# A decoder on one NeuronCore: cross attention by pairs of heads, one local exponential per tile, and other prices in the planner

## The chip, the cores and the metric

The kernel runs on one core of a Trainium2 chip. The metric is the device time of one execution in microseconds. The time before is the median of three runs.

## The reference

1,024 tokens (4 batches of 256) with 256 features pass through six blocks, each on a layer norm of the running sum `x` and added to it: a linear attention with decay, four experts chosen by token number, a product-key memory of 2,025 rows, a local attention, a cross attention, and a mixture of sixteen experts. The change concerns the fourth and fifth:

```python
# local attention: 8 heads of 64, blocks of 16 tokens, causal within a block
qh = einsum('bsd,dhk->bshk', qb, wq) + bq        # kh, vh alike
scores = where(causal, einsum('bqhk,bshk->bhqs', qh / sqrt(64), kh), -1e9)
ctx = einsum('bhqs,bshk->bqhk', softmax(scores), vh)
# cross attention: 16 heads of 16, all 1024 tokens of the context
attn = softmax(einsum('bhqd,bhkd->bhqk', fq_sym(q * scale), fq_sym(k)))
out = einsum('bhqk,bhkd->bhqd', fq_unsigned(attn), fq_sym(v)) @ Wp + bp
```

`fq_sym` and `fq_unsigned` round to 8 bits and back.

## The kernel before

The tokens lie in eight tiles of 128, one token to a partition. Everything up to the mixture of experts is written as Python generators ("streams") that yield wherever another stream may take over: `front(b)` for each batch (the first three blocks up to the indices of the memory), `fetches` (512 indirect DMAs on POOL, 64 for each tile, in 64 groups of eight with three `g` buffers), `weigh` (DVE multiplies and sums the fetched rows with `hb`, ACT takes a tanh, PE adds the weighted rows into `accs` by 16 matmul instructions of 128*32), `turn` and `free` (change of memory pools), `locals_`, `all_queries`, three copies of `units`, `cross_out` and `routes`.

**The order** is written out while the program is built. `Clock.weave` keeps a modelled time for every engine and repeatedly runs the stream whose next step can start first (ties go by rank). `Clock.note` prices each instruction from its shape; `COLUMN` is the price of a column of TensorE in microseconds, 0.00085 at first and 0.0015 from the turn on. On the chip each engine works off its queue in that order; the prices only set the order. A group of fetches may be issued once the group three ahead of it has been added up, and is taken to have landed 8 us after its issue.

**Cross attention** works a unit (a tile and a head) at a time. PE makes the scores, 128 x 1,024, by two bf16 matmuls with 64 rows of contraction (a head's 16 features in several bf16 terms); even heads lie on partitions 0 to 63 and odd ones on 64 to 127. DVE takes the maximum `mx` and a bias `nb`; ACT writes the exponential `e` as 8-bit integers, with its row sums; PE transposes `e` (four 8-bit values at a time as f32), ACT spreads it to bf16 (`qqT`), and PE adds eight products with `vi` into `accs`. Three streams `units(k, 3)` take every third unit. Scores need two adjoining PSUM banks. After the turn seven banks are shared: two such pairs, and three single ones for everything else. A unit gives its pair back after its exponential. Tile t+1 may add into `accs` once `cross_out` has taken tile t's sums (`ao`). Queries of tile t need its local attention, and their buffers the end of cross attention of tile t-2; local attention needs the tile's gathered sum.

**Local attention** of a tile computes all 128 x 128 scores of a head in f32 and masks all but the token's own block of 16. `qh` and `kh` hold even heads on partitions 0 to 63 and odd heads on 64 to 127; two forked streams `half(0)` and `half(1)` each do scores, mask, maximum, four exponentials with row sums, division, four transposes and four products for their four heads.

After `weave` comes the mixture of experts: sorting by expert (from line 1257), 24 row tiles by `up` and `down`, and the gathering of the two results of every token, on an order that does not come from the planner.

The names and lines that matter: `Clock.note` (line 81), `Banks.find` (176), `turn` (828), `local_attention` (902), `units` (1051), the list of streams (1241). In the profile every planned instruction has line 77, the helper that records it, so groups are told apart by tile names.

Of the kernel before, what the change touches and what calls it, by code (L numbers as in the profile page):

```python
# [21 lines left out]
P = 128  # L22
D = 256
NT = 8
# [27 lines left out]
class Clock:  # L52
# [4 lines left out]
    COLUMN = 0.00085  # L57
# [9 lines left out]
    class _Engine:  # L67
# [3 lines left out]
        def __getattr__(self, op):  # L71
            emit = getattr(self.engine, op)

            def timed(*args, **kw):
                out = args[0] if args else kw["out"]
                self.clock.note(self.name, op, out, args, kw)
                return emit(*args, **kw)  # L77

            return timed

    def note(self, engine, op, out, args, kw):
# [81 lines left out]
class Banks:  # L163
# [12 lines left out]
    def find(self, n):  # L176
# [3 lines left out]
        sets = self.pairs if n == 2 else [(k,) for k in self.free if k >= self.single]  # L180
# [24 lines left out]
def decoder(ctx, tc, a, out):  # L205
# [622 lines left out]
    def turn():  # L828
# [12 lines left out]
        A.bk = load(wb, "bk", [P, 4])  # L841
        A.wv = load(wb, "wv", [AW + 1, AH * AW])
# [5 lines left out]
        A.work = ctx.enter_context(tc.tile_pool(name="work", bufs=1))  # L848
        A.q3 = A.work.tile([P, XH, 4, XD], BF16, name="q3", tag="q3")
# [11 lines left out]
        ck.COLUMN = 0.0015  # L861
# [40 lines left out]
    def local_attention(t):  # L902
# [537 lines left out]
```

## Time and profile before

| | |
|---|---|
| Median of three runs | 1300.18 us (1290.26 to 1305.13) |
| The profiled execution | 1261.94 us, span 1260.2 us |
| Mean granted TensorE clock | 0.708 |
| Indices of the first tile ready / first gather | 111 / 112 us |
| Turn of the memory pools | about 404 us |
| First cross scores / last write of `ao` | 493 / 1117 us |
| Last gather issued / last gathered sum added | 971 / 998 us |
| Sorting by expert begins / experts' first gather | 1137 / 1147 us |

In a group's line the columns are: line, engine, operation, tile written <- tiles read, shapes and count; then busy time and mean ns of one; then the engine's idle time just before them and what ended it. In a table of stretches each engine has its busy time and the number of instructions; then follow the granted clock, the DMA engines' busy share and GB/s. An f32 matmul shows as two instructions, a transpose as one. Ends of matmuls are modelled, so PE's busy time is a guide more than a measure.

### The profile page before, as it was taken

How to read it: one execution, taken by the hardware profiler on the slowest of the kernel's cores; microseconds unless marked ns; L12 is line 12 of the kernel's file. 1: busy time of each engine (PE TensorE's matmuls, PEld its weight loads, DVE VectorE, ACT ScalarE, POOL GpSimd, SP SyncE). 2: the span in 40 equal slices, each digit the busy share in tenths (PEclk: the TensorE clock that was granted, in tenths of full speed). 3: DMA queues.
4: the chain of work that ended last, by engine and by line, in shares of the span. 5: the costliest groups of instructions: out<-in, count | busy, mean ns of one | idle time of the engine just before them, and what ended most of it. 6: DMA issues, size and time to landing. Idle time of an engine off the chain costs nothing. (4 is left out here: it accounts for less than half of the span.)

```text
span 1260.2 us, 15565 instructions
## 1 busy us (share of the span) xinstructions
PE 846.4 (67%) x4945; PEld 520.3 (41%) x4945; DVE 821.5 (65%) x2437; ACT 514.4 (41%) x1039; POOL 571.3 (45%) x589
## 2 busy tenths in 40 slices
PE   4672488627834686765688677676786699856990
PEld 3561365414622464333345334343353365323550
DVE  5568667596578458896677775767776767633222
ACT  1241033302301143453575643757456586731220
POOL 2003656575566556576465664655665000002314
PEclk8885588857965877565667866667777566556995
DMA  5012456666556446668665564555665230001323
GB/s 200 1 39 58 135 140 168 188 169 165 138 162 173 134 134 168 172 175 251 167 173 160 162 182 134 149 147 145 179 168 159 87 136 1 5 4 47 84 65 107
DMA packets 68640, 164.67 MB, mean 131 GB/s; under 512 B 15131, under 2 KB 32780, under 8 KB 68557
## 3 DMA queue, kind: packets, MB, share of 16 engines
q0 software_dynamic: 34688, 105.94, 29.9%
q1 hardware_dynamic: 33868, 57.72, 16.6%
q8 instruction: 40, 0.66, 0.2%
q14 instruction: 44, 0.35, 0.1%
HBM read 156.93 MB, written 6.68 MB: 130 GB/s over the span
## 5 line engine op out<-in xcount | busy, mean ns | idle before, releaser
L77 POOL DMA_INDIRECT g<-in_table,idxT x512 | 524.7, 1025 | 438.2 <-issue 153.4
L77 DVE TENSOR_REDUCE mx<-bank 128x1 f32<-128x1024 f32 x128 | 155.8, 1217 | 65.9 <-PE bank L77 51.7
L77 ACT ACTIVATE e<-bank,nb,qs_q 128x1024 uint8<-128x1024 f32 x128 | 154.3, 1206 | 56.1 <-DVE nb L77 22.0
L77 PE MATMUL accs<-g,blk 128*32 128x256 f32 x1024 | 103.9, 542 | 96.5 <-DVE blk L77 69.8
L77 ACT CAST qqT<-bank 128x1024 bf16<-128x1024 uint8 x128 | 127.6, 1010 | 87.9 <-PE bank L77 52.1
L77 PE MATMUL bank<-kT,qT 64*128 64x512 bf16 x256 | 104.2, 518 | 20.8 <-ACT e L77 15.4
L1312 POOL DMA_INDIRECT xr<-xs,smap x24 | 22.7, 948 | 189.5 <-DVE smap L1299 148.4
L77 PEld LDWEIGHTS accs<-g,blk 128*32 128x32 f32 x1024 | 34.5, 141 | 147.3 <-DVE blk L77 77.1
L77 PE MATMUL bank<-ident,e 128*128 128x128 f32 x256 | 72.6, 387 | 32.1 <-ACT e L77 19.0
L77 PE MATMUL accs<-vi,qqT 128*128 128x16 bf16 x1024 | 47.5, 174 | 56.6 <-ACT qqT L77 34.9
L77 DVE TENSOR_TENSOR g<-g,hb 128x1024 f32<-128x1024 f32 x64 | 78.3, 1223 | 8.7 <-issue 5.5
L77 PEld LDWEIGHTS <-qqT 128*128 128x128 bf16 x1024 | 39.8, 103 | 103.7 <-ACT qqT L77 58.9
L77 DVE TENSOR_REDUCE z<-g 128x8 f32<-128x1024 f32 x64 | 78.1, 1220 | 2.2
L77 PEld LDWEIGHTS bank<-ident,e 128*128 128x128 f32 x256 | 36.0, 185 | 85.6 <-issue 35.1
L77 ACT ACTIVATE th<-u 128x16 f32<-128x16 f32 x64 | 13.9, 218 | 90.8 <-DVE u L77 82.0
L77 PE MATMUL bank<-ident,ln_xn 128*128 128x128 f32 x96 | 25.0, 378 | 33.3 <-ACT ln_xn L77 17.1
L77 ACT ACTIVATE ln_xn<-x,ln_nmr,ln_rstd 128x256 f32<-128x256 f32 x48 | 27.0, 595 | 37.4 <-DVE ln_nmr L77 33.1
L77 PE MATMUL bank<-xnT,w_w_up 128*128 128x256 f32 x128 | 35.8, 441 | 7.6 <-ACT xnT L77 4.3
L1321 PE MATMUL ph<-w,xrT 128*128 x96 | 38.9, 513 | 1.8 <-DVE xrT L1318 1.7
L77 PE MATMUL bank<-w_ctxT,aT 128*128 128x256 f32 x128 | 34.3, 421 | 6.7 <-issue 5.1
L77 DVE TENSOR_SCALAR nb<-mx,nsq,ln 128x1 f32<-128x1 f32 x128 | 34.9, 273 | 4.6
L1325 DVE TENSOR_TENSOR hd<-hd,ph 128x176 f32<-128x176 f32 x24 | 8.0, 337 | 42.9 <-ACT hd L1324 42.9
(293 smaller groups left out, 1686.3 us busy)
## 6 DMA issues: line engine op xcount, KB each, us to landing
hb<-hdram SPq DMA_DIRECT2D x128, 256.0 KB
g<-in_table,idxT POOLq DMA_INDIRECT x512
w<-in_w SPq DMA_DIRECT2D x16, 352.0 KB
ys<-yr SPq DMA_DIRECT2D x24, 128.0 KB
w_w2a<-in_w SPq DMA_DIRECT2D x1, 2048.0 KB
x<-in_x SPq DMA_DIRECT2D x8, 128.0 KB
w_ctxT<-in_ctxT SPq DMA_DIRECT2D x1, 1024.0 KB
w_w_up<-in_w_up SPq DMA_DIRECT2D x1, 1024.0 KB
```

The lines of the kernel that those rows point to most:

```text
L77: return emit(*args, **kw)
L1312: nc.gpsimd.indirect_dma_start(out=xr, out_offset=None, in_=xs, in_offset=bass.IndirectOffsetOnAxis(ap=smap[:, i:i + 1], axis=0))
L1321: nc.tensor.matmul(ph.rearrange("p j n -> p (j n)"), xrT[:, k, :], w13[:, bass.ds(e, 1), k, :], start=(k == 0), stop=(k == 1))
L1325: nc.vector.tensor_tensor(hd, hd, ph[:, 1, :], ALU.mult)
```

## The change

Cross attention takes heads by pairs. A unit is now a tile and two heads; it waits until all four banks of the two bank pairs are free, takes them, and issues the four score matmuls with the heads alternating, so that neighbours use different halves of the array's rows. Then it forks into two streams `weighted_sum`, one for each head, which do what followed before. Two streams of pairs take the place of three of single heads. `mx` and `nb` have six buffers in place of four, `e` six in place of three.

Local attention is one stream for all eight heads. The products with `wqk`, the scores and the products with `vh` are issued with their two halves alternating. The masked scores are reduced, by a maximum over the eight blocks of columns, to the 16 columns that belong to the token's own block (`sc`, 128 x 8 x 16); subtracting the maximum, the exponential, the sum and the division happen there, and a product with the 0/1 mask `seen` spreads the result out to 128 columns again. `qh` gets its bias and factor in one instruction with a bias `bq8` that is scaled beforehand, and `cT` is copied whole.

The planner's prices change: `COLUMN` is 0.000525 and then 0.0006, an f32 product is priced at four columns each of at least 128, a transpose in f32 at three, products of 32 output rows at one, bf16 at one; products marked `halves` at 0.55 of that; ACT and DVE prices depend on tensors given as scalars and on row sums.

```diff
-    COLUMN = 0.00085
+    COLUMN = 0.000525
...
                 out = args[0] if args else kw["out"]
                 self.clock.note(self.name, op, out, args, kw)
+                kw.pop("halves", None)
                 return emit(*args, **kw)
...
         n, late = math.prod(out.shape[1:]), 0.11
         if engine == "tensor":
-            wide = (args[2] if op == "matmul" else args[1]).dtype == F32
-            cost, late = max(0.11, n * self.COLUMN) if wide else max(0.03, n * self.COLUMN / 2), 0.17
-            if out.shape[0] == 32:
-                cost = max(0.06, n * self.COLUMN / 4)
+            late = 0.17
+            wide, c = (args[2] if op == "matmul" else args[1]).dtype == F32, self.COLUMN
+            if not wide:
+                cost = max(0.03, n * c)
+            elif op == "transpose":
+                cost = 3 * n * c
+            elif out.shape[0] == 32:
+                cost = n * c
+            else:
+                cost = 4 * c * max(n, P)
+            if kw.pop("halves", False):
+                cost *= 0.55
         elif engine == "scalar":
             scaled, summed = hasattr(kw.get("scale"), "tensor"), "accum_out" in kw
-            cost = 0.06 + n * 0.00083 + 0.23 * (scaled or summed) + 0.06 * (scaled and summed)
+            cost = 0.07 + n * 0.00083 + 0.12 * (scaled or hasattr(kw.get("bias"), "tensor")) + 0.2 * summed
         elif engine == "gpsimd":
             cost = 1.23
         elif op in ("max", "max_index", "tensor_reduce"):
             src = args[1] if op != "max_index" else args[2]
-            cost = (0.15 if op == "max_index" else 0.085) + 0.00104 * math.prod(src.shape[1:])
+            cost = (0.24 if op == "max_index" else 0.085) + 0.00104 * math.prod(src.shape[1:])
         elif op == "reciprocal":
             cost = 0.05 + 0.0064 * n
         elif op == "tensor_tensor_scan":
             cost = 0.1 + 0.0022 * n
+        elif op in ("tensor_scalar", "tensor_copy"):
+            cost = 0.085 + 0.09 * sum(hasattr(x, "tensor") for x in args[2:]) + 0.00054 * n
         else:
-            cost = 0.085 + (0.00054 if op in ("tensor_scalar", "tensor_copy") else 0.00104) * n
+            cost = 0.085 + 0.00104 * n
...
-        sets = self.pairs if n == 2 else [(k,) for k in self.free if k >= self.single]
+        sets = (self.pairs if n == 2 else [sum(self.pairs, ())] if n == 4 else
+                [(k,) for k in self.free if k >= self.single])
...
+        A.bq8 = wb.tile([P, 4], F32, name="bq8", tag="bq8")
+        nc.vector.tensor_scalar(A.bq8, A.bq, 0.125, None, ALU.mult)
...
+        A.seen = A.work.tile([P, P // ABLK, ABLK], F32, name="seen", tag="seen")
+        nc.vector.tensor_scalar(A.seen, cmask, -0.5, None, ALU.is_ge)
...
-        ck.COLUMN = 0.0015
+        ck.COLUMN = 0.0006
...
         se_.activation(vT[0:AW, :], pqk[0:AW, 1, :], AF.Identity, bias=A.conv_bv)
         bank.give(pqk)
         yield "tensor", None
+
+        p = []
+        for part in range(2):
+            p.append((yield from bank.take([P, 4, P])))
+        for m in range(4):
+            for part in range(2):
+                lo = part * AW
+                te_.matmul(p[part][:, m, :], A.wqk[lo:lo + AW, m * P:(m + 1) * P], qk[lo:lo + AW, :],
+                           start=True, stop=True, halves=True)
+        yield "vector", None
+
         qh = work.tile([P, 4, P], F32, name="qh", tag="qh")
+        ve_.scalar_tensor_tensor(qh, p[0], 0.125, bc(A.bq8, 2, P), ALU.mult, ALU.add)
+        bank.give(p[0])
         kh = work.tile([P, 4, P], F32, name="kh", tag="kh")
-        for part, lo in ((0, 0), (1, AW)):
-            p = yield from bank.take([P, 4, P])
-            for m in range(4):
-                te_.matmul(p[:, m, :], A.wqk[lo:lo + AW, m * P:(m + 1) * P], qk[lo:lo + AW, :], start=True, stop=True)
-            yield "vector", None
-            if part == 0:
-
-                for m in range(4):
-                    ve_.tensor_scalar(qh[:, m, :], p[:, m, :], A.bq[:, m:m + 1], 0.125, ALU.add, ALU.mult)
-            else:
-                ve_.tensor_tensor(kh, p, bc(A.bk, 2, P), ALU.add)
-            bank.give(p)
-            yield "tensor", None
+        ve_.tensor_tensor(kh, p[1], bc(A.bk, 2, P), ALU.add)
+        bank.give(p[1])
+        yield "tensor", None
+
+        psc = []
+        for o in range(2):
+            psc.append((yield from bank.take([P, 4, P])))
+        for m in range(4):
+            for o in range(2):
+                te_.matmul(psc[o][:, m, :], qh[o * AW:(o + 1) * AW, m, :], kh[o * AW:(o + 1) * AW, m, :],
+                           start=True, stop=True, halves=True)
+        yield "vector", None
+        pr = work.tile([P, AH, P // ABLK, ABLK], F32, name="pr", tag="pr")
+        for o in range(2):
+            ve_.tensor_tensor(pr[:, 4 * o:4 * o + 4].rearrange("p m g j -> p m (g j)"), psc[o],
+                              bc(cmask.rearrange("p g j -> p (g j)"), 1, 4), ALU.add)
+            bank.give(psc[o])
+
+        sc = work.tile([P, AH, ABLK], F32, name="sc", tag="sc")
+        ve_.tensor_reduce(sc, pr.rearrange("p h g j -> p h j g"), AX.X, ALU.max)
+        sm = work.tile([P, AH], F32, name="sm", tag="sm")
+        ve_.tensor_reduce(sm, sc, AX.X, ALU.max)
+        ve_.tensor_tensor(sc, sc, bc(sm, 2, ABLK), ALU.subtract)
+        yield "tensor", None
         pv = yield from bank.take([P, AH * AW])
         te_.matmul(pv, vT, A.wv, start=True, stop=True)
         yield "scalar", None
+        se_.activation(sc, sc, AF.Exp)
         vh = work.tile([P, AH * AW], F32, name="vh", tag="vh")
         se_.copy(vh, pv)
         bank.give(pv)
-        cT = work.tile([P, 4, P], F32, name="cT", tag="cT")
-
-        def half(o):
-
-            psc = yield from bank.take([P, 4, P])
-            for m in range(4):
-                te_.matmul(psc[:, m, :], qh[o * AW:(o + 1) * AW, m, :], kh[o * AW:(o + 1) * AW, m, :], start=True, stop=True)
-            yield "vector", None
-            pr = work.tile([P, 4, P], F32, name="pr", tag="pr", bufs=2)
-            ve_.tensor_tensor(pr, psc, bc(cmask.rearrange("p g j -> p (g j)"), 1, 4), ALU.add)
-            bank.give(psc)
-            nm = work.tile([P, 4], F32, name="nm", tag="nm", bufs=2)
-            ve_.tensor_reduce(nm, pr, AX.X, ALU.max, negate=True)
-            yield "scalar", None
-            sm = work.tile([P, 4], F32, name="sm", tag="sm", bufs=2)
-            for m in range(4):
-                se_.activation(pr[:, m, :], pr[:, m, :], AF.Exp, bias=nm[:, m:m + 1], accum_out=sm[:, m:m + 1])
-            yield "vector", None
-            ve_.reciprocal(sm, sm)
-            ve_.tensor_tensor(pr, pr, bc(sm, 2, P), ALU.mult)
-            yield "tensor", None
+        yield "vector", None
+        ve_.tensor_reduce(sm, sc, AX.X, ALU.add)
+        ve_.reciprocal(sm, sm)
+        ve_.tensor_tensor(sc, sc, bc(sm, 2, ABLK), ALU.mult)
+        ve_.tensor_tensor(pr, bc(sc, 2, P // ABLK), bc(A.seen, 1, AH), ALU.mult)
+        yield "tensor", None
+        prf = pr.rearrange("p h g j -> p h (g j)")
+        prT = []
+        for o in range(2):
             tp = yield from bank.take([P, 4, P])
             for m in range(4):
-                te_.transpose(tp[:, m, :], pr[:, m, :], ident)
+                te_.transpose(tp[:, m, :], prf[:, 4 * o + m, :], ident)
             yield "scalar", None
-            prT = work.tile([P, 4, P], F32, name="prT", tag="prT", bufs=2)
-            se_.copy(prT, tp)
+
+            prT.append(work.tile([P, 4, P], F32, name="prT", tag=("qh", "kh")[o]))
+            se_.copy(prT[o], tp)
             bank.give(tp)
             yield "tensor", None
-            pc = yield from bank.take([P, 4, P])
-            for m in range(4):
+        pc = yield from bank.take([P, 4, P])
+        for m in range(4):
+            for o in range(2):
                 h = 2 * m + o
-                te_.matmul(pc[o * AW:(o + 1) * AW, m, :], vh[:, h * AW:(h + 1) * AW], prT[:, m, :], start=True, stop=True)
-            yield "scalar", None
-            se_.copy(cT[o * AW:(o + 1) * AW], pc[o * AW:(o + 1) * AW])
-            bank.give(pc)
-
-        yield "tensor", None
-        yield from ck.fork(half(0), half(1))
+                te_.matmul(pc[o * AW:(o + 1) * AW, m, :], vh[:, h * AW:(h + 1) * AW], prT[o][:, m, :],
+                           start=True, stop=True, halves=True)
+        yield "scalar", None
+        cT = work.tile([P, 4, P], F32, name="cT", tag="cT")
+        se_.copy(cT, pc)
+        bank.give(pc)
         yield "tensor", None
...
     def units(k, n):
 
+
+        for j in range(k, NT * XH // 2, n):
+            t, c = 2 * j // XH, j % (XH // 2)
+            yield "tensor", lambda: qready.get(t)
+            while bank.find(4) is None:
+                yield "tensor", (bank, 4)
+            psc = []
+            for o in range(2):
+                psc.append((yield from bank.take([P, T], n=2)))
+            for n_ in range(2):
+                for o in range(2):
+                    hr = slice(o * 64, o * 64 + 64)
+                    te_.matmul(psc[o][:, n_ * 512:(n_ + 1) * 512], QT[t][hr, c, :], kT[hr, c, n_ * 512:(n_ + 1) * 512],
+                               start=True, stop=True, halves=True)
+            yield "vector", None
+            yield from ck.fork(*[weighted_sum(t, 2 * c + o, psc[o]) for o in range(2)])
+
+    def weighted_sum(t, h, psc):
         work = A.work
-        for j in range(k, NT * XH, n):
-            t, h = j // XH, j % XH
-            yield "tensor", lambda: qready.get(t)
-            o, c = h % 2, h // 2
-            hr = slice(o * 64, o * 64 + 64)
-            psc = yield from bank.take([P, T], n=2)
-            for n_ in range(2):
-                te_.matmul(psc[:, n_ * 512:(n_ + 1) * 512], QT[t][hr, c, :], kT[hr, c, n_ * 512:(n_ + 1) * 512],
-                           start=True, stop=True)
-            yield "vector", None
-            mx = work.tile([P, 1], F32, name="mx", tag="mx", bufs=4)
-            ve_.tensor_reduce(mx, psc, AX.X, ALU.max)
-            nb = work.tile([P, 1], F32, name="nb", tag="nb", bufs=4)
-            ve_.tensor_scalar(nb, mx, NSQ[t][:, h:h + 1], ln255, ALU.mult, ALU.add)
-            yield "scalar", None
-
-            e = work.tile([P, T], U8, name="e", tag="e", bufs=3)
-            se_.activation(e, psc, AF.Exp, bias=nb, scale=SQ[t][:, h:h + 1], accum_out=SUMS[t][:, h:h + 1])
-            bank.give(psc)
-
-            yield "tensor", lambda: None if weighted[0] == 2 else 0.0 if t == 0 else summed.get(("o", t - 1))
-            weighted[0] += 1
-
-            tp = yield from bank.take([P, 2, P])
-            for o in range(2):
-                te_.transpose(tp[:, o, :], e.bitcast(F32)[:, o * P:(o + 1) * P], ident)
-            yield "scalar", None
-            qqT = work.tile([P, 8, P], BF16, name="qqT", tag="qqT", bufs=2)
-            se_.copy(qqT.rearrange("p (o j) q -> p o j q", o=2), tp.bitcast(U8).rearrange("p o (q j) -> p o j q", j=4))
-            bank.give(tp)
-            yield "tensor", None
-            for s in range(NT):
-                te_.matmul(accs[:, 1, h * XD:(h + 1) * XD], qqT[:, s, :], vi[:, s, h * XD:(h + 1) * XD],
-                           start=False, stop=(s == NT - 1), skip_group_check=True)
-            weighted[0] -= 1
-            nunits[t] += 1
-            if nunits[t] == XH:
-                summed[("x", t)] = ck.end
+        mx = work.tile([P, 1], F32, name="mx", tag="mx", bufs=6)
+        ve_.tensor_reduce(mx, psc, AX.X, ALU.max)
+        nb = work.tile([P, 1], F32, name="nb", tag="nb", bufs=6)
+        ve_.tensor_scalar(nb, mx, NSQ[t][:, h:h + 1], ln255, ALU.mult, ALU.add)
+        yield "scalar", None
+
+        e = work.tile([P, T], U8, name="e", tag="e", bufs=6)
+        se_.activation(e, psc, AF.Exp, bias=nb, scale=SQ[t][:, h:h + 1], accum_out=SUMS[t][:, h:h + 1])
+        bank.give(psc)
...
-                  Stream(weights()), Stream(locals_()), Stream(all_queries(), rank=0), *[Stream(after_turn(units, k, 3)) for k in range(3)],
+                  Stream(weights()), Stream(locals_()), Stream(all_queries(), rank=0), *[Stream(after_turn(units, k, 2)) for k in range(2)],
```

More of the change, by code (lines that the diff above doesn't have):

```diff
@@ new lines, in weighted_sum @@
+    def weighted_sum(t, h, psc):
+        work = A.work
+        mx = work.tile([P, 1], F32, name="mx", tag="mx", bufs=6)
[6 more added lines that the diff above has]
+        bank.give(psc)
+        yield "tensor", lambda: None if weighted[0] == 2 else 0.0 if t == 0 else summed.get(("o", t - 1))
+        weighted[0] += 1
+        tp = yield from bank.take([P, 2, P])
+        for o in range(2):
+            te_.transpose(tp[:, o, :], e.bitcast(F32)[:, o * P:(o + 1) * P], ident)
+        yield "scalar", None
+        qqT = work.tile([P, 8, P], BF16, name="qqT", tag="qqT", bufs=2)
+        se_.copy(qqT.rearrange("p (o j) q -> p o j q", o=2), tp.bitcast(U8).rearrange("p o (q j) -> p o j q", j=4))
+        bank.give(tp)
+        yield "tensor", None
+        for s in range(NT):
+            te_.matmul(accs[:, 1, h * XD:(h + 1) * XD], qqT[:, s, :], vi[:, s, h * XD:(h + 1) * XD],
+                       start=False, stop=(s == NT - 1), skip_group_check=True)
+        weighted[0] -= 1
+        nunits[t] += 1
+        if nunits[t] == XH:
+            summed[("x", t)] = ck.end
```

## The prediction

> **What bounds the kernel now.** I read the page's busy shares first, then the busy time of each engine between the ends of neighbouring tiles' cross attention (the writes of `ao`), then the groups, the waits, and the chain.
>
> ```profile
> PE 846.4 (67%) x4945; PEld 520.3 (41%) x4945; DVE 821.5 (65%) x2437; ACT 514.4 (41%) x1039; POOL 571.3 (45%) x589
> ...
> core 0: us, PE busy (x) PEld busy (x) DVE busy (x) ACT busy (x) POOL busy (x), PEclk, DMA share, GB/s
> 490.00:591.00 101.00, 64.01 (x432) 33.65 (x432) 85.82 (x264) 47.89 (x96) 67.14 (x64) 0.58 0.68 189
> 848.00:926.00 78.00, 55.66 (x402) 30.28 (x400) 58.04 (x152) 45.69 (x89) 47.32 (x47) 0.72 0.58 162
> 926.00:1005.00 79.00, 56.02 (x402) 31.20 (x399) 58.33 (x121) 49.03 (x90) 31.17 (x31) 0.70 0.45 126
> 1005.00:1065.00 60.00, 55.72 (x344) 36.59 (x344) 41.10 (x115) 43.88 (x82) 0.00 (x0) 0.66 0.26 89
> 1065.00:1117.00 52.00, 39.58 (x218) 16.88 (x216) 31.27 (x72) 38.29 (x58) 0.00 (x0) 0.51 0.01 3
> ```
>
> No engine is full over the span. Cross attention runs without a break from 490 to 1117 us, one tile after the other: 77 to 101 us a tile while gathers still run, then 60, then 52. In the 60 us stretch PE is busy for 55.7: there it is the bound. Before that PE and DVE are each some 70 to 75% busy, and in-order queues lose the rest:
>
> ```profile
> L77 POOL DMA_INDIRECT g<-in_table,idxT x338 | 344.9, 1020 | 223.2 <-issue 101.0 <-PE accs L77 75.9 <-PE bank L77 31.3
> L77 DVE TENSOR_REDUCE mx<-bank 128x1 f32<-128x1024 f32 x128 | 155.8, 1217 | 65.9 <-PE bank L77 51.7 <-remote 6.4 <-PE accs L77 4.1
> L77 ACT ACTIVATE e<-bank,nb,qs_q 128x1024 uint8<-128x1024 f32 x128 | 154.3, 1206 | 56.1 <-DVE nb L77 22.0 <-DVE blk L77 8.9 <-DVE ln_rstd L77 8.7
> L77 PE MATMUL bank<-kT,qT 64*128 64x512 bf16 x256 | 104.2, 518 | 20.8 <-ACT e L77 15.4 <-issue 4.0 <-ACT qT L77 1.3
> L77 DVE TENSOR_SCALAR nb<-mx,nsq,ln 128x1 f32<-128x1 f32 x128 | 34.9, 273 | 4.6
> L77 ACT ACTIVATE pr<-pr,nm 128x128 f32<-128x128 f32 x64 | 24.8, 393 | 3.1 <-DVE nm L77 3.1
> L77 PE MATMUL bank<-kh,qh 64*128 64x128 f32 x128 | 24.7, 429 | 0.0
> L77 PE MATMUL bank<-qk,w_wqk 64*128 64x128 f32 x128 | 22.3, 321 | 11.0 <-ACT qk L77 9.3 <-DVE qh L77 1.1 <-issue 0.5
> L77 PE MATMUL bank<-prT,vh 128*64 128x128 f32 x128 | 20.5, 326 | 0.2 <-ACT xnT L77 0.2
> ```
>
> (Groups between 405 and 1117 us.) The reader sees three circles of waiting: POOL for g buffers that PE has not yet consumed (75.9 + 31.3 us), DVE's maximum for PE's scores (51.7), and PE for ACT's results. The chain that ended last, between 998 and 1140 us, is 36.0% PE on banks, 8.2% the exponential, 7.7% the maximum, 6.5% the cast `qqT`.
>
> **What the Trainium skill says.** "TensorEngine Tiling (Array Packing)", Theoretical Speedup: contractions of at most 64 gain up to 2x when two row tiles work at once; its Gotcha 1 asks that row tiles write different PSUM banks, which the two `psc` do. "TensorE: Matmul & The Clock Gate", Part 3: four row tiles measured 3.07x, and matmuls stay strictly in order, so the partners have to be neighbours in the queue. The trace agrees for column groups: 16 matmuls `accs<-g` of 128*32 take 1.07 us together (at 411 and 713 us) where one shows 542 ns. Neighbouring row tiles occur nowhere in it. Part 1 of the same page says an idle PE falls back to half clock; the trace agrees (0.51 in the last stretch, 0.7 before). Freed PE time may therefore come back as lower clock.
>
> **The change, part by part.**
>
> *Scores in pairs.* 256 matmuls, 104.2 us busy, 0.81 us a head. At 2x they would take 52. I take 1.8x, an estimate between the page's 3.07 of 4 and its 2 of 2: 58 us, 46 less, 5.8 a tile. Ends: nothing gained (no overlap), or 26 us lost if each of the 256 weight loads (101 ns) were exposed by the alternation; and 52 gained.
>
> *Local attention's products by halves.* 24.7 + 22.3 + 20.5 = 67.5 us; at 1.8x, 30 less, 3.7 a tile (ends 0 and 34).
>
> *One local exponential.* Out go 64 exponentials (24.8) and their 64 accumulator reads (12.2); in come 8 of 128 elements at 0.39, 3.1. The 16 half copies of `cT` (9.3) become 8 whole ones at 0.58 (4.6). ACT loses 38.6 us, 4.8 a tile.
>
> *Local softmax on DVE.* Before: qh 9.0, kh 5.5, mask 11.0, nm 11.0, reciprocals 2.7, `pr`x`sm` 11.1, 50.3 in all. After: qh 8 x 0.69, kh 5.5, mask 11.0, the block maximum over 1024 elements 8 x 1.22 (row `mx`; its strided read is not in the trace, I allow +-3), four small operations 8 x 4 x 0.22, reciprocals 1.4, the spreading product 8 x 1.22: 50.1. Nothing gained, though it is one chain now where two halves alternated between DVE and ACT. `bq8` and `seen` are one instruction each at the turn.
>
> *Pairs take all four wide banks.* This adds a wait: the next pair's scores stand on PE until both exponentials of the pair ahead are done, and behind them stand weighing, local products and transposes; POOL waits for that weighing. From the rows, an undisturbed pair: scores 1.1, hop 0.1, two maxima with `nb` 2 x 1.49, second exponential 1.2 with its read 0.2, hop 0.15: 5.7 us. The last tile now takes 52/16 = 3.25 a head, 6.5 a pair, with three heads in flight on two slots. Alone the lock costs nothing. In the gather stage other work cuts in. DVE spends 58 us a tile (848 to 1005), of which maxima and `nb` are 24, so 34 are foreign, 4.3 a pair. If all of it fell inside the chain, 5.7 + 4.3 = 10.0 us a pair, 80 a tile, what it takes today (78, 79). PE's foreign work counts on top (rival one).
>
> *Three streams become two* of two heads each, with six `e` buffers: up to four heads in flight. No cost of its own.
>
> *Prices of the order.* The planner prices an f32 product of 256 columns at 0.22 us before the turn and 0.38 after it; the trace has two instructions of some 0.44 each, pipelined to 0.5 to 0.8. Eight `accs` products are priced 0.48 (later 0.77), trace 1.07 for sixteen instructions; `nb` 0.086, trace 0.273. New: 0.54/0.61, 1.08/1.23, 0.265. No instruction goes; what can go is waiting of the kind above. Between 405 and 1117 us DVE waits 51.7 + 18.4 + 13.9 = 84 us for banks. I take a fifth, 17 us, and for the front to 405 us nothing. Ends: 70 gained (two thirds of POOL's 107 us), 30 lost, since any new order also makes new bad meetings.
>
> **The sum,** against the profiled execution (span 1260.2, time 1261.94). Freed time counts by its share of the chain where no engine is full.
> - 490 to 1005, six tiles: PE 9.5 x 0.36 = 3.4, ACT 4.8 x 0.2 = 1.0; 4.4 x 6 = 26.
> - 1005 to 1065, PE-bound: 8 of the 9.5.
> - 1065 to 1117: 8 pairs x 5.7 + the last pair's transposes, casts and products 3.4 = 49 for 52: 3.
> - Order: 17. After 1117 nothing: the experts are untouched.
>
> That is 54 us: 1262 becomes 1208, a ratio of 0.957. The runs' median, 1300.18, lies 3% above the profiled time; the same ratio gives **1244**.
>
> **The rivals.** *The lock costs more than it saves (slower).* PE's foreign work in the gather stage is 56 less 13 for scores, 43 us a tile, 5.4 a pair. With 4.3 from DVE that is 9.7 us that can cut into a pair's chain; the break-even is 10.0 - 5.7 = 4.3, less than half of it. If half plus a little (5.6) does, a pair takes 11.3, a tile 90 instead of 79: 11 x 7 = 77 lost, the tail's and the order's 28 and some local work kept: about +40: 1302, or 1341 in the median. For it: one maximum behind a 2.45 us weighing delays two heads. Against: DVE finds foreign work while ACT finishes the pair.
> *The gather sets the pace (within 1%).* The last sum of gathered rows is at 998 us. If it stays there, only 8 + 3 us of the tail are gained: 1288. For it: POOL's own minimum is 112 + 512 x (1.025 + 0.30) = 790. Against: the last issue is at 971, so POOL waits on others and follows them.
> *The order was the main loss (much faster).* If two thirds of POOL's 107 us go and cross attention follows: 54 - 17 + 70 = 107, 1262 to 1155, 1190 in the median.
>
> **How the numbers follow.** Forecast (1215 to 1275) 0.46; main loss in the order 0.25; gather's pace 0.10; lock 0.19. A change under about 1% can't be told from none in this kernel. Faster 0.71, same 0.10, slower 0.19. The range of 8 in 10 goes past the fast rival's 1190 to 1168, which leaves out 0.06, and up to 1325, which leaves out the greater part of the slow one, 0.14. The forecast's own range is 1215 to 1275.
>
> **What would show it.** Scores: four neighbouring `kT,qT` matmuls within 1.0 to 1.2 us, the group's busy time at 55 to 60. Local: `pr` exponentials gone, `sc` x8 at 0.39. Lock: PE's wait on ACT `e` ahead of `kT,qT`, now 15.4 us, grows without the tiles' 77 to 79 us growing; above 85 a tile the slower rival holds. Order: POOL's waits on PE below 107 and the last sum of gathered rows ahead of 998 us. The forecast is wrong if row tiles don't overlap, if tiles take as long as before, or if the front up to 405 us moves by over 15 us either way.

## The result, and the profile after

Twenty runs of each kernel, taken together: 1294.3 us before (1277.65 to 1312.03), 1306.95 us after (1293.75 to 1321.42). The ratio is **1.0121, with an interval of 1.0088 to 1.0154**: 1.2% slower, where 1244 us and a ratio of 0.957 were forecast. (The ratio leaves out runs more than 1.5% above the quickest of the same kernel; the medians of all twenty give 1.0098.) Against the median of the three runs shown before, 1300.18, the new median is 0.5% up.

The profiled execution of after took 1311.05 us (span 1309.3), 49 us more than that of before. That pair overstates the change: before's profiled execution was 32 us quicker than its own median, after's 4 us slower than its own. First the views that answer to those of before, then a pair of traces that agrees with the medians.

Busy shares over the span in the first profile of after, from its page:

```profile
PE 811.9 (62%) x4945; PEld 501.8 (38%) x4945; DVE 825.3 (63%) x2423; ACT 485.0 (37%) x911; POOL 567.2 (43%) x589
```

The table of stretches of the same profile, from one write of `ao` to the next: the first tile and the last four (length; busy time of PE, PEld, DVE, ACT and POOL with instruction counts; granted clock, DMA share, GB/s):

```profile
573.00:664.00 91.00, 53.54 (x400) 27.52 (x400) 56.48 (x114) 42.30 (x71) 57.86 (x57) 0.65 0.76 205
...
942.00:1006.00 64.00, 48.98 (x395) 27.26 (x392) 53.49 (x145) 46.84 (x78) 8.96 (x9) 0.82 0.46 142
1006.00:1067.00 61.00, 45.53 (x325) 30.13 (x324) 41.64 (x95) 40.95 (x64) 0.00 (x0) 0.61 0.00 1
1067.00:1122.00 55.00, 43.73 (x287) 25.00 (x284) 40.77 (x112) 42.40 (x68) 0.00 (x0) 0.66 0.02 6
1122.00:1166.00 44.00, 32.78 (x210) 16.94 (x208) 28.12 (x67) 34.22 (x53) 0.00 (x0) 0.50 0.01 4
```

The work went: PE is 35 us less busy over the span, ACT 29. The last tiles got shorter: 55 and 44 us where 60 and 52 stood. But cross attention starts at 573 instead of 492 us and ends at 1166 instead of 1117. Its length fell from 625 to 593, its start moved by 81, and the difference, 49, is the whole difference of the spans.

The groups between the turn and the last `ao` (447 to 1166 us) of the same profile:

```profile
L78 POOL DMA_INDIRECT g<-in_table,idxT x308 | 313.9, 1019 | 197.7 <-issue 85.4 <-PE accs L78 60.7 <-PE bank L78 21.2
L78 DVE TENSOR_REDUCE mx<-bank 128x1 f32<-128x1024 f32 x128 | 155.8, 1217 | 82.3 <-PE bank L78 64.2 <-ACT qk L78 10.0 <-PE accs L78 4.4
L78 ACT ACTIVATE e<-bank,nb,qs_q 128x1024 uint8<-128x1024 f32 x128 | 154.1, 1207 | 36.0 <-DVE nb L78 19.4 <-remote 5.5 <-DVE mx L78 4.9
L78 PE MATMUL bank<-kT,qT 64*128 64x512 bf16 x256 | 71.3, 526 | 25.8 <-ACT e L78 16.1 <-issue 5.2 <-ACT qT L78 4.2
L78 PE MATMUL bank<-kh,qh 64*128 64x128 f32 x128 | 15.0, 376 | 8.2 <-DVE kh L78 4.1 <-DVE blk L78 3.9 <-ACT qqT L78 0.2
L78 DVE TENSOR_REDUCE sc<-pr 128x128 f32<-128x1024 f32 x8 | 15.0, 1874 | 0.3
L78 PE MATMUL bank<-qk,w_wqk 64*128 64x128 f32 x128 | 13.3, 317 | 8.7 <-ACT qT L78 4.0 <-ACT hT L78 3.3 <-issue 1.4
L78 PE MATMUL bank<-prT,vh 128*64 128x128 f32 x128 | 12.1, 335 | 1.4 <-ACT prT L78 0.8 <-issue 0.5
```

Row tiles do overlap: the scores' busy time fell from 104.2 to 71.3, local attention's three products from 67.5 to 40.4. PE's wait for the exponential ahead of the scores is 16.1 us against 15.4: this trace shows no sign of a lock from taking four banks at once.

**Two groups of chips.** The kernel before takes 1270 to 1300 us on some chips and 1142 to 1143 us on others; each chip on record was used in one session, so chip and session can't be told apart. In the longer runs' traces engines wait for nothing that the profile can name ("issue", or "remote"). These waits of the first profile of after, from the view of waits, stand for many:

```profile
PE bank L78 <- issue: 63.2, 39, 7.3
...
ACT qqT L78 <- remote: 22.8, 7, 7.4
```

(us in total, times, the longest.) All such waits of PE, DVE and ACT sum to 51, 71 and 164 us in the first profile of before, and to 79, 91 and 226 in that of after. On a quick chip the same kernel has none on PE, 3 us on DVE and 0.3 on ACT, at the same instruction durations. Both kernels were therefore run again on such a chip ("repeat"): 1143.05 us before, 1150.45 after, **1.0062 (1.0042 to 1.0082)**. Their profiled executions, 1143.19 and 1150.43, agree with the medians, so the causes are read there.

Stretches of the repeat of before: indices ready to turn, turn to first cross queries, a stretch common to both kernels, and the last two tiles:

```profile
118.00:367.00 249.00, 160.02 (x902) 112.53 (x901) 201.51 (x679) 66.68 (x149) 174.52 (x171) 0.77 0.67 183
367.00:433.00 66.00, 56.18 (x369) 43.05 (x368) 48.22 (x165) 26.57 (x69) 45.62 (x46) 0.97 0.69 185
433.00:889.00 456.00, 354.19 (x2539) 196.19 (x2536) 376.94 (x947) 286.48 (x544) 294.55 (x294) 0.69 0.67 184
889.00:948.00 59.00, 54.27 (x343) 35.74 (x339) 40.95 (x115) 43.64 (x82) 0.00 (x0) 0.68 0.26 90
948.00:998.00 50.00, 36.29 (x219) 15.62 (x216) 31.18 (x72) 38.16 (x58) 0.00 (x0) 0.59 0.01 3
```

The same of the repeat of after:

```profile
124.00:388.00 264.00, 171.54 (x1002) 119.41 (x1004) 215.19 (x709) 68.45 (x157) 203.86 (x197) 0.80 0.74 202
388.00:485.00 97.00, 52.01 (x368) 34.22 (x360) 71.22 (x282) 19.66 (x51) 74.46 (x75) 0.69 0.74 200
433.00:889.00 456.00, 308.29 (x2481) 176.19 (x2482) 377.69 (x987) 259.37 (x441) 286.85 (x279) 0.69 0.67 185
...
906.00:961.00 55.00, 43.74 (x287) 25.08 (x284) 40.73 (x112) 42.39 (x68) 0.00 (x0) 0.66 0.02 6
961.00:1005.00 44.00, 32.73 (x210) 16.93 (x208) 28.11 (x67) 34.22 (x53) 0.00 (x0) 0.50 0.01 4
```

Cross attention starts 52 us later (433 to 485), is 45 us shorter (564 to 519) and ends 7 later; the spans differ by 7.2. Turn to first queries takes 97 us instead of 66, with the same number of PE instructions (368 and 369) but 282 on DVE instead of 165. What those are, in the groups up to the first queries of each:

```profile
L77 POOL DMA_INDIRECT g<-in_table,idxT x216 | 220.5, 1021 | 95.2 <-issue 65.3 <-PE accs L77 22.8 <-PE bank L77 4.3
...
L77 DVE TENSOR_REDUCE z<-g 128x8 f32<-128x1024 f32 x25 | 30.5, 1220 | 0.9
L77 DVE MAX8 mx<-sim 128x8 f32<-128x45 f32 x74 | 14.1, 191 | 3.2 <-ACT sim L77 3.2
```

(before, 118 to 433 us) and

```profile
L78 POOL DMA_INDIRECT g<-in_table,idxT x275 | 283.9, 1032 | 192.7 <-ACT pT L78 108.8 <-issue 77.4 <-PE accs L78 2.2
...
L78 DVE TENSOR_REDUCE z<-g 128x8 f32<-128x1024 f32 x33 | 40.3, 1220 | 1.1
L78 DVE MAX8 mx<-sim 128x8 f32<-128x45 f32 x96 | 18.4, 191 | 0.2 <-ACT sim L78 0.2
```

(after, 118 to 485 us; the 108.8 us on `pT` are the wait for the first gather, which before lies ahead of the window.) Eight more groups of gathered rows (a tile has eight) have been weighed before cross attention starts, and 22 more of the key maxima of the last batch's front have been taken, in a window that is 52 us longer. POOL hardly waits for PE there any more (2.2 us named against 27.1), and the last tile's gathered sum is added at 818 instead of 882 us. The time is shifted from inside cross attention to ahead of it.

### The profile page after: what moved, and what is told of

Its sections match the earlier page's. It is cut to its first block, busy times and chain, and to the rows that moved or that the text cites. A ratio compares the mean times of both kernels' runs of the same rounds, so it can differ in the third digit from the quotient of the medians.

```text
span 1309.3 us, 15403 instructions
## 1 busy us (share of the span) xinstructions
PE 811.9 (62%) x4945; PEld 501.8 (38%) x4945; DVE 825.3 (63%) x2423; ACT 485.0 (37%) x911; POOL 567.2 (43%) x589
## 4 chain that ended last, share of the span: by engine, by line
PE 35%; DVE 32%; issue 10%; ACT 10%; another core or an unknown queue 8%; DMA 2%; POOL 1%; DVEq 0%; POOLq 0%; ACTq 0%
PE bank L78 25%; DVE mx L78 5%; PE accs L78 5%; ACT e L78 3%; DVE z L78 3%; DVE g L78 3%; ACT qqT L78 3%; PE ph L1360 3%; DVE mi L78 2%; DVE oh L78 1%; POOL g L78 1%; PE py L1377 1%; DVE sc L78 1%; DVE ln_nt L78 1%
## 5 line engine op out<-in xcount | busy, mean ns | idle before, releaser
L78 DVE TENSOR_REDUCE mx<-bank 128x1 f32<-128x1024 f32 x128 | 155.8, 1217 | 82.3 <-PE bank L78 64.2
L78 PE MATMUL accs<-g,blk 128*32 128x256 f32 x1024 | 109.7, 546 | 91.8 <-DVE blk L78 30.1
L78 PE MATMUL bank<-kT,qT 64*128 64x512 bf16 x256 | 71.3, 526 | 25.8 <-ACT e L78 16.1
L78 PEld LDWEIGHTS bank<-ident,e 128*128 128x128 f32 x256 | 34.9, 183 | 97.6 <-issue 55.4
L78 PE MATMUL bank<-w_ctxT,aT 128*128 128x256 f32 x128 | 38.9, 460 | 26.5 <-DVE aT L78 26.5
L78 ACT ACTIVATE th<-u 128x16 f32<-128x16 f32 x64 | 13.9, 216 | 110.4 <-DVE u L78 77.4
L78 PEld LDWEIGHTS bank<-w_ctxT,aT 128*128 128x128 f32 x128 | 28.4, 231 | 36.1 <-DVE aT L78 29.4
L78 DVE MAX8 mx<-sim 128x8 f32<-128x45 f32 x128 | 24.5, 191 | 25.2 <-ACT sim L78 25.2
L78 PE MATMUL bank<-xp,w_conv_w 128*128 128x128 f32 (+1 forms) x192 | 33.0, 337 | 8.9 <-issue 5.6
```

## The experiments

The first four take the change apart by its prices; the kernel before took 1142.38 us beside them. The question was whether the 1.2% came from the new order, from the lock, or from what pairs and local attention really cost.

**Prices alone**, on the kernel before:

```diff
-    COLUMN = 0.00085
+    COLUMN = 0.000525
...      # Clock.note as in the change; units and local_attention as before
-        ck.COLUMN = 0.0015
+        ck.COLUMN = 0.0006
```

> The kernel before with the new prices alone, from start to end. Theory A (the new prices put the front in a worse order: the turn moves from 404 to about 447 us, the first cross exponential by some 80 us): the turn lies after 435 us, 1.02 to 1.04 times the time before. Theory B (the prices help, the four-bank lock of the pairs costs): the turn moves little, 0.97 to 0.99 times.

1155.79 us, **1.0143 (1.0108 to 1.0179)**. Turn at 388, first queries at 493, last gathered sum at 816, cross attention 517 us long: the shift of the whole change, with neither pairs nor the new local attention in it. From the turn to the first queries:

```profile
388.00:493.00 105.00, 55.52 (x388) 36.48 (x380) 75.27 (x294) 24.01 (x70) 80.56 (x81) 0.73 0.73 203
```

**Pairs and local attention with the old prices**:

```diff
-    COLUMN = 0.000525
+    COLUMN = 0.00085
...      # Clock.note as in the kernel before; halves left unpriced
-        ck.COLUMN = 0.0006
+        ck.COLUMN = 0.0015
```

> The changed kernel (pairs and one local exponential) with the old prices throughout. Theory A: the turn is back at 400 to 410 us and the later gain stays: 0.96 to 0.98 times the time before. Theory B: the lock is still there: 1.01 or more.

1151.62 us, **1.0090 (1.0056 to 1.0125)**. Turn 368, first queries 438, last gathered sum 872: the start is back, and the gain of 2 to 4% that theory A expected is not there. Cross attention takes 570 us against 564, although PE works 44 us less over the span (768.2 against 812.1) and ACT 26 less.

**The new prices on one side of the turn only**, the rest as changed:

```diff
-    COLUMN = 0.000525
+    COLUMN, MEASURED = 0.00085, False
...      # Clock.note holds both sets of prices, and takes the new ones if MEASURED
-        ck.COLUMN = 0.0006
+        ck.COLUMN, ck.MEASURED = 0.0006, True
```

(This is the late variant; the early one starts with the new prices and goes back to the old ones at the turn.)

> The changed kernel with the old prices up to the turn and the new ones after it. Theory A: the turn is at 400 to 410 us, cross attention of a tile takes 5 us less than before on average: 0.95 to 0.98. Theory B: as the changed kernel, about 1.01.

> The changed kernel with the new prices up to the turn and the old ones after it. Theory A: the turn is at about 447 us and the loss remains: 1.00 to 1.03. Theory B: about 1.01 as well; this run tells, together with the one with late prices alone, which half of the order loses.

Late: 1138.62 us, **0.9985 (0.9968 to 1.0002)**. Early: 1151.75, 1.0085 (1.0049 to 1.0120). Late prices take 1.0090 to 0.9985, some 12 us: the gain that was expected of the order exists (first queries 446, length 542). Put in early as well they take 0.9985 to 1.0062: the start moves by another 39 us and only 23 come back in length. Without the late ones the early ones cost nothing beyond the old-price kernel (start +22, length -21). The two do not add: 1.0090 less the effect of each would be 0.998.

**The repeat, and each of the two kernel edits alone.** Pairs alone: `units` and `weighted_sum`, two streams, `e` with three buffers, all else as before. Local alone: the new `local_attention`, `bq8` and `seen`, all else as before. Both with the old prices.

```diff
-                  ... *[Stream(after_turn(units, k, 3)) for k in range(3)],
+                  ... *[Stream(after_turn(units, k, 2)) for k in range(2)],      # pairs alone
```

> The kernel before once more, for a profile of it on the chip of these runs. All theories: the same time as the kernel before; the waits that end in nothing the profile shows (on PE 51 us, on ACT 159 us in the first trace) are absent if they belong to the other chip, and the turn lies at about 366 us, where the two runs with the old front have it.

> The changed kernel, timed and profiled on the chip of these runs. The run with early prices alone took 1.0085 and the one with late prices alone 0.9985 of the time before. Theory A (the front's new order costs some 1%, the later order gains 1%, pairs and local exponential nothing together): 0.998 to 1.01. If the two halves of the order don't add up: 1.012 as in the first measurement or more.

> The kernel before with the pairs of heads alone (old prices, old local attention; three buffers for e, because the old local attention leaves no room for six). Theory C (the four-bank lock eats what the side by side scores give): 1.005 to 1.02 times the time before, with kT,qT busy 68 to 71 us instead of 104. Theory L (the local attention as one chain loses): 0.98 to 0.995.

> The kernel before with the new local attention alone (old prices, single heads). Theory C: 0.98 to 0.995, as ACT is freed of 38 us and PE of some 30. Theory L: 1.005 to 1.02.

Beside 1143.05: the repeat of before 1143.43, of after 1150.45 (1.0062); pairs alone 1144.28, **1.0024 (1.0009 to 1.0038)**; local alone 1145.65, 1.0027 (1.0008 to 1.0047). Cross attention is 564 us long in both, as in the repeat of before. In pairs alone, the common stretch, then the first six tiles and the last two:

```profile
433.00:889.00 456.00, 334.20 (x2557) 199.88 (x2556) 375.07 (x948) 282.36 (x538) 298.94 (x295) 0.70 0.70 195
434.00:899.00 465.00, 340.53 (x2598) 205.02 (x2599) 381.48 (x961) 290.18 (x562) 298.24 (x294) 0.70 0.69 191
899.00:999.00 100.00, 73.32 (x491) 39.82 (x490) 67.10 (x173) 77.90 (x122) 0.00 (x0) 0.64 0.01 5
```

and the scores in its view of groups:

```profile
L78 PE MATMUL bank<-kT,qT 64*128 64x512 bf16 x256 | 70.0, 518 | 9.3 <-ACT e L78 8.1 <-ACT qT L78 1.1
```

PE has 20 us less to do in the 456 us, and its wait for the exponential is 8.1 us where the repeat of before had 19.6. Neither reaches the end. The six tiles take 465 us where the repeat of before took 456, and the last two 100 instead of 109: what the tail gains the six tiles lose, and some 4 us of DVE's work and of ACT's moved from the tail into them. With both kernel edits at the old prices it is 474 and 96. Both runs lie between the ranges of the two theories that their expectations set against each other.

DVE's busy time in the common stretch stays between 370 and 389 us in these eight kernels, where PE's goes from 308 to 354. That made a new theory: DVE, 83% busy there, alone hides what the others save.

**DVE's load.** `nb` (34.9 us in all on DVE) goes to ACT in the kernel before, the changed one and the one with late prices, and is made twice on DVE in the kernel before.

```diff
-        ve_.tensor_scalar(nb, mx, NSQ[t][:, h:h + 1], ln255, ALU.mult, ALU.add)
         yield "scalar", None
+        se_.activation(nb, mx, AF.Identity, bias=ln255, scale=NSQ[t][:, h:h + 1])
```

> The kernel before with nb computed twice on DVE. Theory D: 35 us more on DVE, 20 to 35 us of it seen: 1.017 to 1.03. Theory C: 0.27 us more in each round of two or more that overlap: 1.00 to 1.01.

> The kernel before with the bias nb computed on ACT (one more activation of 128 x 1 for each head) and no longer on DVE. Theory D (between the turn and the end of the gathers DVE is the bound, 0.83 busy, and what PE and ACT are freed of doesn't count): DVE loses 35 us, some 80 of 128 heads of it in that stage, so 20 to 30 us go: 0.975 to 0.985 times the time before. Theory C (the rounds of score, maximum, exponential and the banks they hold are the bound): the round keeps its length, 0.995 to 1.01.

> The changed kernel with nb on ACT. Theory D: 20 to 30 us less than the changed kernel, so 0.98 to 0.99 times the kernel before. Theory C: as the changed kernel, 1.00 to 1.01.

> The changed kernel with the old prices up to the turn, the new ones after it, and nb on ACT. Theory D: 0.97 to 0.98 times the kernel before, the fastest so far, since freed ACT time takes up nb. Theory C: 0.995 to 1.005, as with late prices alone.

Before took 1142.34 here. Twice: 1163.84, **1.0197 (1.0144 to 1.0249)**, 22 us for 35 more on DVE. Off DVE: 0.9973 (0.9955 to 0.9991) on the kernel before, 3 us; 0.9963 (0.9944 to 0.9981) on the changed kernel, 11 us below its 1.0062; and 1130.3 us, **0.9910 (0.9881 to 0.9938)**, with late prices, 9 below its 0.9985. The last is quicker than both kernels of this study. The answer is lopsided: DVE work added costs two thirds of itself, DVE work taken away gives a tenth to a third. ACT pays 49.4 us for these (386 ns each), and each edit gives another order, so the loads were next taken away in an order held fixed.

**Half of the maximum.** The maximum of the scores is taken over the first 512 columns; the kernel leaves out the other half.

```diff
-        ve_.tensor_reduce(mx, psc, AX.X, ALU.max)
+        ve_.tensor_reduce(mx, psc[:, 0:512], AX.X, ALU.max)
```

> The kernel before with the maximum of the cross scores taken over the first 512 of 1,024 columns; it leaves out the other half, so DVE has some 68 us less to do. Theory D: 0.965 to 0.985 times the kernel before, after which PE or the rounds bind. Theory P: 0.99 to 1.00.

> The changed kernel with the maximum over half the columns, as in the run beside it. Theory D: with DVE relieved the change's freed PE and ACT time shows: 0.93 to 0.955 of the kernel before, that is 0.96 to 0.98 of the relieved kernel before. If the four-bank rounds bind instead: no better than the relieved kernel before.

On a chip where before took 1270.06: 1.0160 (1.0077 to 1.0243) and 1.0162 (1.0088 to 1.0237), where neither theory had expected a loss. Slower with 68 us less on DVE, since the planner prices the shorter maximum and lays out another order. So the order had to be kept: the planner was told the full maximum, and the half was issued.

```diff
-        ve_.tensor_reduce(mx, psc, AX.X, ALU.max)
+        ck.note("vector", "tensor_reduce", mx, (mx, psc, AX.X, ALU.max), {})
+        nc.vector.tensor_reduce(mx, psc[:, 0:512], AX.X, ALU.max)
```

> The kernel before in its own order, with the maximum over the first 512 columns only (it leaves out the other half) and the planner told of the whole. Theory D (DVE is the bound in the middle): of 68 us some 43 lie in the stage where DVE is 0.83 busy; 20 to 45 us go, 0.96 to 0.985 times the kernel before. Theory R (in-order rounds over three engines, no single bound): 10 us or less, 0.99 to 1.00, or slower, as with half the maximum before.

> The changed kernel in its own order, with the maximum over half the columns and the planner told of the whole. Theory D: freed PE and ACT time shows once DVE is relieved, so more goes than in the run beside it: 0.94 to 0.965 of the kernel before. Theory R: each pair's round loses 2 x 0.53 us on its path where three single heads overlap, so 0.97 to 0.99, again more than in the run beside it; no more than beside it: the rounds don't bind either.

Before took 1270.11. The kernel before: 1259.22, **0.9916 (0.9886 to 0.9946)**, 11 us for 68 (the group falls from 155.8 to 87.7). The changed kernel: 1290.39, 1.0103 (1.0033 to 1.0174), within the interval of its full version (1.0121, from other chips). DVE alone isn't the cover either. The changed kernel gained no more from it than the kernel before; by its expectation that speaks against the rounds of four banks as the bound, too, as far as runs on different chips can be compared.

**Alternation and start.** The four score matmuls one head after the other; and a front for the third batch that may start 30 us earlier by the planner's clock, meant to bring the turn forward.

```diff
-            for n_ in range(2):
-                for o in range(2):
+            for o in range(2):
+                for n_ in range(2):
...
-        ... (3.0, 0.0, 0.0, 0.0)[b] ...
+        ... (3.0, 0.0, 30.0, 0.0)[b] ...
```

> The changed kernel with the four score products of a pair issued head after head, in the same order otherwise. Theory D (DVE masks it): kT,qT busy is back at 95 to 104 us and the time stays that of the changed kernel, 1.004 to 1.010 times the kernel before. Theory P (PE counts, and the scores' length is in every pair's round): some 0.5 us for each of 64 pairs, of which the last three tiles alone see 12 us: 1.015 to 1.03.

> The changed kernel with a lead of 30 us in the planner for the front of the third batch, which gates the turn. Theory A (the late turn is the loss): the turn moves from 387 to 365 us or earlier and the time to 0.985 to 0.997. Theory D: what the front gains the gathered sums lose on DVE, DVE's idle time up to the end stays near 196 us: 1.00 to 1.01.

Not alternated: 1302.67 us, 1.0269 (1.0190 to 1.0347) beside 1270.06; the changed kernel was not run on that chip, so this doesn't say what alternation is worth. The group's busy time is 77.4, not the 95 or more expected, 6 us above the alternated one: no test of what 30 us of PE would do. The timelines of PE say why. Three sets in the kernel before, then one in the run without alternation:

```profile
492.84 1.04 PE L77 MATMUL bank<-kT,qT 64*128 64x512 bf16 x4 [1.10 <-ACT qT L77]
517.59 1.03 PE L77 MATMUL bank<-kT,qT 64*128 64x512 bf16 x2
1066.47 1.88 PE L77 MATMUL bank<-kT,qT 64*128 64x512 bf16 x4
724.72 1.04 PE L78 MATMUL bank<-kT,qT 64*128 64x512 bf16 x4
```

The first is an even and an odd head, queued one after the other; its four matmuls start at 0, 6, 401 and 408 ns. The second is a lone head, whose two matmuls use the same rows: 0 and 400 ns. So in the first set the odd head's first matmul started beside the even head's first, ahead of the even head's second that stood before it in the queue. The third set is two even heads: 0, 400, 826 and 1253 ns. The last, head after head in the changed kernel, starts at 0, 7, 400 and 407. The two halves of the array overlap, then, once two heads of different halves stand together in the queue and both bank pairs are free; the alternation is not needed for it. And PE does not keep strictly to the planner's order.

The lead: 1347.99 us, **1.0644 (1.0575 to 1.0714)**. The turn came at 419, the first gathered sum at 346 us instead of near 251: it moved everything and isolated nothing. It shows only how far an order can throw this kernel.

## Why the prediction failed

**"For the front to 405 us nothing"** is the step that set the sign. It named its own bound, 15 us either way. In the repeat the turn moved by 21 us and the start of cross attention by 52. The prediction quoted the prices on both sides of the turn and then booked their effect on one side; but they order the front as well. Taken alone, on the kernel before, the prices move the start by 60 us (493 against 433) and lose 1.4%; with the old prices kept up to the turn, the loss of the change is gone (0.9985).

**"Freed time counts by its share of the chain where no engine is full"** (26 us in six tiles) is the step that removed the gain. Pairs alone and local alone left the length of cross attention as it was, within 1 us, and both at the old prices made it 6 us longer. In the six tiles, where 26 us were to go, pairs alone took 9 us more and both edits 18 more. A share of the chain is what an engine held in one execution; that it is not what comes out if its work shrinks is what these runs show. The reason is only argued: each of PE, ACT and DVE may be the last to arrive at some hand-over.

**"PE-bound: 8 of the 9.5"** and the last tile's 3 came closest. In the first pair the last two tiles went from 60 and 52 to 55 and 44: 13 where 11 was predicted; in the repeat 59 and 50 became 55 and 44, 10 in all. The last tile's eight pairs take 44 us; 49 was the estimate. But by then the start had been lost.

**Order, 17 gained.** The sign depends on where: about 12 us gained with new prices after the turn, given back with them before it. What would show it came true, "the last sum of gathered rows ahead of 998": 978 in the first pair, 818 against 882 in the repeat; and the end of cross attention did not follow.

**Sizes.** Scores: 1.8x was assumed, 55 to 60 us; measured 71, or 1.4x. The overlap as such is the full 2x: the unbroken set above takes 1.04 us for two heads, and the lone head at 517.59 us 1.03. But pairs are often split in the queue (23 of 64 in the repeat, one and three), because the second head's bank pair comes free only after the second exponential ahead. The timeline of PE in the repeat of after:

```profile
904.31 0.58 PE L78 MATMUL bank<-kT,qT 64*128 64x512 bf16 x1 [0.81 <-ACT e L78]
905.50 1.01 PE L78 MATMUL bank<-kT,qT 64*128 64x512 bf16 x3 [0.60 <-ACT e L78]
```

One score goes alone, three follow 1.2 us later. The prediction took two things too strictly here. That matmuls stay strictly in order, so that partners have to be neighbours in the queue, it had from the Trainium skill ("TensorE: Matmul & The Clock Gate", Part 3); the starts above contradict it. And neighbouring row tiles did occur in the trace of before, at 492.84 us for one.

Local products: 27 us gained, 30 predicted. Local exponential: 0.31 us, 0.39 predicted. Block maximum: 1.87 us each where 1.22 was predicted, 5.2 us more for all eight, beyond the 3 us allowed. ACT: 29 us less by the page, 38.6 predicted; the sum added the old exponentials (24.8) and their reads (12.2), but these overlap in the trace of before and cover 28.0 us together. The freed PE time did not come back as a lower clock: it is 0.69 in the common stretch of both repeats. Nor does the clock follow PE's busy share in the prediction's own rows: 0.51 at 76% in the last stretch, 0.72 at 71% from 848 to 926.

**The rivals.** The changed kernel shows no lock: PE's wait for `e` ahead of the scores is 19.6 us before and 18.2 after in the repeat, and no tile of it takes over 81 us against the 85 named. At the old prices it is not excluded: pairs alone lengthened the six tiles, two of them took 91 and 103 us (89 at most in the repeat of before), and yet PE's wait for `e` fell to 8.1. In the first pair two tiles did take 99 and 103 us, but PE's wait there stood still (15.4 and 16.1) and the mean tile fell from 78 to 74 us. The gather's pace is refuted by the repeat: gathered sums ended 64 us earlier and cross attention went on for 187 us after them. The order as main loss had the right part of the kernel in view and the sign of one half of it. The slower outcome had a chance of 0.19, all of it on the lock; that a new order loses by itself stood in the working only as one end of a range, "30 lost".

**What stays open.** Why freed time is not worth its share is open. The guess that is left is that queues in a fixed order on three engines set the length: relieving PE (20 to 50 us), ACT (29 us) or DVE (35, 68 us) gave at most a third of it and often nothing. That is argued, not shown; no run let the engines take their work in another order than the planner's while all else stayed. Not run: late prices on the kernel before, without pairs. What the unexplained waits on some chips are is open too, and with them why the loss is 1.2% in the first pair and 0.6% in the repeat.

## What to carry to other kernels

A planner's prices are an edit to every stage that it orders: before costing them, ask which stage gets its work earlier and which later, and predict the start of the critical stage as well as its length. Where no engine is full and each works through a fixed queue, don't count on work taken from one engine until a run shows its worth; here 51 us of PE and 29 us of ACT bought none, and other orders of the same work moved the time by -1% to some +5%. To measure what an engine's load costs, keep the order: let the planner price the old instruction and issue the new one.

## What the runs showed of the hardware

- A maximum over 1024 f32 elements in SBUF whose innermost step is 16 elements (64 bytes) took 1874 ns; `z<-g`, over 1024 contiguous ones, 1220. The Trainium skill, "SBUF — State Buffer", Specifications (TRN2), says that each crossing to a new 16-byte line costs; the trace agrees in direction, and the page gives no size for it. The two reductions also differ in the number of their results (128 and 8 a partition), so the stride's part is not separated.
- The same kernel took 1142 to 1143 us on three chips and 1270 to 1300 in the runs elsewhere, 11 to 14% more, at equal instruction durations, with waits in the traces of the longer ones that end in nothing the profile names.
- Matmuls of 64 rows on different halves of the array's rows overlapped fully (four in 1.04 us, where four on one half took 1.88), also where the queue held them head after head.
- A multiply-add on 128x1 with two values from each partition took 273 ns on DVE and 386 ns on ACT.
